# Causal attention on VectorE, TensorE and GpSimd: the sine product taken from PSUM, the products of the key chunks set apart, the last three for both heads at once

## The chip, the cores and the metric

The kernel runs on one core of one Trainium2 chip. The metric is the device time of one execution in microseconds (us). The engines carry the profile's names: PE is TensorE (PEld its weight loads), DVE is VectorE, ACT is ScalarE, POOL is GpSimd, and SP is the queue that issues most DMAs.

## The reference, cut to what matters

Everything is fp32. The input x is 4 batches of 1024 rows of 256. An attention with 16 heads of 64, rotary positions and a causal mask comes first, then a residual and a layer norm, then a mixture of 16 experts (3 for each row) with another residual and norm. The change touches the attention alone:

```python
q = _rope(q, sin, cos)
k = _rope(k, sin, cos)
att = jnp.einsum('bhqd,bhkd->bhqk', q, k) * scale      # scale = 1/8
att = jnp.where(mask, att, -inf)
att = softmax(att)
y = jnp.einsum('bhqk,bhkd->bhqd', att, v)
return y @ W_out.T + b_out
...
y_lo = x_lo * cos + x_hi * sin                          # in _rope
y_hi = x_hi * cos - x_lo * sin
```

So a rotated q or k is the projection times a sine table plus the projection with its halves swapped times a cosine table.

## The kernel before, in words

**Tiling.** The attention runs over 32 pairs n: 4 batches times 8 pairs of heads. The two heads of a pair lie in partitions 0 to 63 and 64 to 127. Queries and keys of a batch are 8 chunks of 128 each. A pair has six slots k, and its query chunks come from the longest row to the shortest, `chunks = [(7,), (6,), (5,), (4,), (3, 2), (1, 0)]` (L410): query chunk 7 sees 8 key chunks, query chunk 0 sees one.

**The steps of a pair.** In the slots of the pair before it, `project` (L200) makes q and k, transposed: two matmuls of 512 columns for each half of the positions (L214), then an activation of ScalarE from PSUM to SBUF that adds the bias and, for q, multiplies by SCALE (L218). SP then copies the tile with its 32-row halves swapped (four DMAs, L230). `rotate` (L232) multiplies the projection by the sine table where it stands (L236: on DVE for q, on POOL for k), the swapped copy by the cosine table (L242, POOL), and adds (L245, POOL). `values` (L247) makes v for two pairs at once (L254), copies it out of PSUM (L259, ScalarE) and stores it to a DRAM scratch (L264, SP); `spread` (L271) loads it back as vr with 32 keys of each of four groups on the partitions.

`scores` (L279) multiplies one or two query chunks with all keys that they see (L300, tiles of 64 rows and 128 columns, one for each head), DVE adds the mask and takes the row's extreme from PSUM into SBUF (L308), and ScalarE takes exp with the row's sum (L320). `divide` (L331) takes the reciprocal of the sum on DVE (L334) and multiplies on POOL (L337). Two slots later `turn` (L346) transposes the probabilities in 32x32 blocks on DVE (L357) into two tiles: t_first for key chunks 0 to 3 and t_last for 4 to 7. Each has one buffer.

`product` (L364) does one key chunk j of probabilities times values for all query chunks from j on: 4 blocks u of 32 queries, 2 heads, 4 blocks a of 32 keys, each a matmul with a 32x64 tile of vr as weights and 32 (8 - j) columns (L378); chunk 7 leaves 12 of the 32 out. The trace records each fp32 matmul as two MATMUL and two LDWEIGHTS. The results stay in four PSUM tiles y_ps, one for each a, until all chunks are added. `close` (L386) adds the bias of v and joins the four tiles into yT with four activations of ScalarE (L391), and `out` (L397) multiplies yT with the output weights (L400), a quarter of the rows a call; DVE adds that to the residual (`sum`, L455).

**What sets the order.** PE's instructions stand in the order of the program (`manual_schedule`, L427). Within slot k of pair n they are: for k = 2 the product of chunks 1 and 0 of the pair before and its close; the scores; for k = 0 and 1 the products of chunk 4 and of chunks 3 and 2 of the pair before, for k = 3, 4, 5 those of chunk 7, 6, 5 of this pair; an `out` in slots 0, 3, 4, 5; the projections of the next pair, K0, K1, Q1, Q0 in slots 0 to 3 (0 and 1 are halves of the positions); values in slots 4 and 5. The other engines take what is ready by the order of the program, which `after` (L327) ties with dependencies that mean order alone: the sum behind the first head's transposes, the reciprocals behind the second's, the sine multiplication of q behind the transposes, POOL's rotations behind the divides. The rotation of k is written in slot 2, that of Q1 in slot 3, of Q0 in slot 5.

**PSUM.** [...]four (ps_s) go round among scores, projections, values, out and the router, four (ps_y) hold y_ps. A PE tile in ps_s waits until its buffer's reader is done.

**The MoE part.** The router of a batch (layer norm, routing, table scatters) is spread over slots of later pairs by `plan`; the experts run behind the attention.

## Time and profile before

| what | us |
|---|---|
| median of 3 runs | 1808.53 (1807.02 to 1809.19) |
| the profiled execution | 1897.37 |
| its span | 1895.6 |
| PE busy with matmuls | 1671.1 |
| POOL, DVE, ACT busy | 1191.2, 1169.3, 713.4 |
| mean of a scores reduction L308 over 512 columns without a row so far | 0.685 |
| mean of a transpose L357 | 0.588 |
| mean of an exp L320 | 0.766 |
| mean of a divide L337 | 0.769 |
| mean of a projection matmul L214 | 0.622 |

The span is what the profile covers, 1.8 us less than its execution. Durations of PE rows overlap[...]: how long a step takes is read from the start of one step to the start of the next. A wait in brackets behind a row of a timeline is the idle time before it with the instruction that ended it.

### The profile page before, as it was taken

Reading aid. Unit: us, or ns where it says so; the run is one execution under the profiler, and the core shown is the slowest. Engines: PE = TensorE matmul, PEld = TensorE weight load, DVE = VectorE, ACT = ScalarE, POOL = GpSimd, SP = SyncE. Lnnn points to the kernel's source line nnn. Section 1 sums busy time; section 2 is a strip of 40 time slices with the busy share of each in tenths; the row PEclk is TensorE's granted clock in tenths of the full one; section 3 lists DMA queues with packets and bytes.
Section 4 is the critical chain, followed back from the end, with each engine's and each line's share of the span. In section 5 each row is a group of like instructions: output and inputs, shape, how many; then the busy total and the mean of one; then the engine's idle time right before and its main releaser. Section 6 shows DMA issues by size and latency. Waiting matters only on the chain.

```text
span 1895.6 us, 51958 instructions
## 1 busy us (share of the span) xinstructions
PE 1671.1 (88%) x20920; PEld 1141.3 (60%) x20920; DVE 1169.3 (62%) x3458; ACT 713.4 (38%) x1634; POOL 1191.2 (63%) x1077
## 2 busy tenths in 40 slices
PE   7899999988989898899999798898779799999980
PEld 3466556555555565555555465554458588888870
DVE  4687788868766787886668778766625122223224
ACT  3445454544344444444345443343312122222223
POOL 3776577655667775556776655577536778777542
PEclk9899999999999998999999998999879899999995
DMA  6365445463444556345444643343367689888856
GB/s 178 92 162 141 115 117 128 117 187 94 116 99 98 109 124 184 91 122 115 99 107 99 193 100 92 84 95 90 93 219 192 143 239 249 234 237 228 219 94 266
DMA packets 118168, 272.97 MB, mean 144 GB/s; under 512 B 21874, under 2 KB 72434, under 8 KB 102563
## 3 DMA queue, kind: packets, MB, share of 16 engines
q1 hardware_dynamic: 93122, 239.91, 46.2%
q0 software_dynamic: 24656, 29.68, 8.9%
q8 instruction: 167, 2.74, 0.7%
q14 instruction: 79, 0.64, 0.1%
q10 hardware_dynamic: 144, 0.01, 0.0%
HBM read 183.17 MB, written 52.79 MB: 124 GB/s over the span
## 4 chain that ended last, share of the span: by engine, by line
PE 59%; DVE 17%; issue 10%; DMA 7%; SPq 3%; ACT 2%; POOL 1%; ACTq 0%; DVEq 0%; POOLq 0%
PE y_ps L378 16%; PE ps L874 10%; PE ps L890 10%; PE s L300 8%; PE pp L214 6%; PE oo L400 4%; DVE p L308 4%; DVE t_first L357 4%; PE vv L254 3%; SPq L230 3%; DMA swq<-rotq 3%; DVE t_last L357 3%; ACT p L320 1%; PE ps L862 1%; DVE acc L455 1%
## 5 line engine op out<-in xcount | busy, mean ns | idle before, releaser
L337 POOL TENSOR_SCALAR p<-p,rinv 128x512 f32<-128x512 f32 (+7 forms) x512 | 385.8, 769 | 450.6 <-DVE rinv L334 446.4
L320 ACT ACTIVATE p<-p,nmax 128x512 f32<-128x512 f32 (+7 forms) x512 | 392.0, 766 | 474.2 <-DVE nmax L308 415.8
L300 PE MATMUL s<-rotk,rotq 64*128 64x512 f32 (+3 forms) x1536 | 343.0, 533 | 44.5 <-DVE x2T L578 17.1
L308 DVE CUSTOM_DVE_ANT_0 p<-s,zero 128x512 f32<-128x512 f32 x256 | 165.8, 685 | 246.7 <-PE s L300 242.0
L300 PEld LDWEIGHTS s<-rotk,rotq 64*128 64x128 f32 x1536 | 160.8, 193 | 232.0 <-issue 102.6
L357 DVE STREAM_TRANSPOSE t_first<-p 128x512 f32<-128x512 f32 (+3 forms) x512 | 288.9, 588 | 0.9 <-POOL p L337 0.9
L378 PE MATMUL y_ps<-t_first,vr 32*64 32x160 f32 (+2 forms) x8192 | 250.9, 348 | 28.4 <-issue 25.2
L214 PE MATMUL pp<-xT,wqk 128*128 128x512 f32 x512 | 254.6, 622 | 16.4 <-DVE nmax L308 8.8
L378 PEld LDWEIGHTS y_ps<-t_first,vr 32*64 32x64 f32 x8192 | 181.0, 134 | 110.1 <-issue 79.6
L904 POOL DMA_INDIRECT sums<-y,ids x112 | 178.5, 1594 | 72.2 <-DVE y L900 37.8
L879 ACT ACTIVATE hid<-ps,w 128x256 f32<-128x256 f32 x224 | 93.7, 471 | 333.7 <-issue 264.4
L874 PE MATMUL ps<-xg,w 128*128 128x256 f32 x896 | 210.8, 387 | 8.6 <-issue 5.7
L895 DVE TENSOR_TENSOR y<-ps,w 128x512 f32<-128x512 f32 x56 | 38.7, 691 | 286.5 <-PE ps L890 215.6
L890 PE MATMUL ps<-w,hid 128*128 128x256 f32 x896 | 203.9, 380 | 1.9 <-issue 1.8
L874 PEld LDWEIGHTS ps<-xg,w 128*128 128x128 f32 x896 | 169.6, 195 | 33.3 <-issue 9.1
L890 PEld LDWEIGHTS ps<-w,hid 128*128 128x128 f32 x896 | 169.6, 190 | 25.6 <-issue 2.8
L400 PE MATMUL oo<-wo,yT 128*128 128x256 f32 x512 | 153.4, 425 | 32.9 <-DVE nmax L308 31.3
L378 PE MATMUL y_ps<-t_last,vr 32*64 32x96 f32 (+3 forms) x7424 | 148.4, 257 | 32.9 <-DVE t_last L357 16.3
L378 PEld LDWEIGHTS y_ps<-t_last,vr 32*64 32x64 f32 x7424 | 116.5, 137 | 95.7 <-issue 54.0
L214 PEld LDWEIGHTS pp<-xT,wqk 128*128 128x128 f32 x512 | 94.6, 195 | 109.7 <-issue 67.6
L308 DVE CUSTOM_DVE_ANT_0 p<-s,mask,nmax 128x512 f32<-128x512 f32 (+3 forms) x256 | 130.3, 545 | 0.9 <-issue 0.5
L254 PE MATMUL vv<-wv,xT 128*128 128x256 f32 x512 | 130.1, 401 | 0.0
(150 smaller groups left out, 1985.4 us busy)
## 6 DMA issues: line engine op xcount, KB each, us to landing
vr<-v_d SPq DMA_DIRECT2D x256, 256.0 KB
w<-in_wall_dram SPq DMA_DIRECT2D x56, 1154.0 KB
swq<-rotq SPq DMA_DIRECT2D x256, 64.0 KB
swk<-rotk SPq DMA_DIRECT2D x128, 128.0 KB
v_d<-v SPq DMA_DIRECT2D x128, 128.0 KB
wqk<-in_w_qk_dram SPq DMA_DIRECT2D x32, 256.0 KB
xT<-in_xT_dram SPq DMA_DIRECT2D x8, 512.0 KB
wv<-in_w_v_dram SPq DMA_DIRECT2D x16, 256.0 KB
```

The costliest lines, as they stand in the source:

```text
L214: nc.tensor.matmul(ps, lhsT=wqk[n][:, c, i, :], rhs=xts[b, g][:, c, :], start=(c == 0), stop=(c == DC - 1),)
L254: nc.tensor.matmul(ps[:, u, :], lhsT=xts[b, cc // 2][:, c, ts(cc % 2 * 2 + u, P)], rhs=wv[n][:, c, :], start=(c == 0), stop=(c == DC - 1),)
L300: nc.tensor.matmul(s[:, :n_k], lhsT=rot[n, 0, qc // 4][ts(hh, KD), ts(qc % 4, P)], rhs=k[ts(hh, KD), ds(k0, n_k)], start=True, stop=True,)
L308: order["scores"] = nc.vector.tensor_tensor_reduce(out=probs[n, qc, hh][:, ds(k0, n_k)], in0=s[:, :n_k], in1=mask[:, 512 - n_k :] if last ...
L320: nc.scalar.activation(pr, pr, AF.Exp, bias=m, scale=-1.0, accum_out=rsum[:, hh : hh + 1])
L337: order["divide"] = router.behind = nc.gpsimd.tensor_scalar(pr, pr, rinv[:, hh : hh + 1], 1.0, ALU.mult, ALU.mult)
L357: order["turn"] = router.on_dve = after(nc.vector.transpose(t[:, hh, :, ds(i - 4 * h, n_j, step=step), :], pr[:, ds(512 * h, n_j * P)].rea ...
L378: nc.tensor.matmul(st[n][a][ts(hh, KD), ds(32 * j, 32 * (TC - j))], lhsT=vrs[n, h][ts(a, 32), jh // 2 * 8 + 2 * u + jh % 2, ts(hh, KD)], r ...
L400: nc.tensor.matmul(ps[:, v, :], lhsT=st[n][:, ts(2 * h + v, P)], rhs=wo[n], start=True, stop=True,)
L874: nc.tensor.matmul(ps[:, f - f0, :], lhsT=w[:, ds(c * FF + f * P, P)], rhs=xg[:, c, :], start=(c == 0), stop=(c == DC - 1),)
L890: nc.tensor.matmul(ps[:, h, :], lhsT=hid[:, f, ts(h, P)], rhs=w[:, ds(W2_AT + f * D, D)], start=(f == 0), stop=(f == FC - 1),)
L904: s = behind(nc.gpsimd.indirect_dma_start(out=sums[t % 2], out_offset=bass.IndirectOffsetOnAxis(ap=ids[:, h, i : i + 1], axis=0), in_=y[:, ...
```

## The change

The change has four parts.

1. The sine product is made by DVE straight from the projection's PSUM tile: (projection + bias) x sine in one operation, into the tile of the rotated q or k, ordered behind the reciprocal of the slot. ScalarE's activation still copies projection plus bias to SBUF, now into a tile of its own (`raw`), and only the swap DMAs read that. `rotate` keeps the cosine product and the sum. The scale of the scores moves from q into the reduction on DVE, and the mask is divided by it.
2. The projections are K0, K1, Q1 in slots 0 to 2 and Q0 in slot 5. Q1 is rotated in slot 4, Q0 in slot 0 of its own pair. Values go from slots 4 and 5 to 3 and 4. For pair 0, values of two tiles go from ahead of the loop to its slots 1 and 2, and the first projections are in another order.
3. No two key chunks follow each other on PE: slot 0 has the scores, chunk 4, out, a projection, chunk 3; slot 1 the scores, chunk 2, a projection; slot 2 chunk 1, the scores, chunk 0, the close, a projection. The transposes are ordered by halves of the keys: both heads' t_last, the sum, both heads' t_first.
4. Chunks 7, 6 and 5 (WIDE = 3) use 32x128 tiles of vr with both heads as weights and both heads' probabilities as columns: half as many matmuls with twice the columns. In the result, the quarter that pairs a head's values with its own probabilities is kept for each head; the cross terms land in the other quarters of y_ps, which now uses 512 columns, and are not read. The close has eight activations of 64 partitions.

```diff
...
         rot = {}
-        swps = {}
+        raws, swps = {}, {}
         def project(n, i, g):
             b, p = divmod(n, NP)
             if i == 0:
-                res = rot[n, 0, g] = qkp.tile([P, 512], FP, tag=f"rotq{g}", name="rotq")
-                half, whole = res, True
+                half = rot[n, 0, g] = qkp.tile([P, 512], FP, tag=f"rotq{g}", name="rotq")
+                part = raw = qkp.tile([P, 512], FP, tag="rawq", name="rawq")
+                whole = True
             else:
                 whole = (n, 1) in rot
                 if not whole:
                     rot[n, 1] = qkp.tile([P, T], FP, tag="rotk", name="rotk")
-                res = rot[n, 1]
-                half = res[:, ts(g, 512)]
+                    raws[n] = qkp.tile([P, T], FP, tag="rawk", name="rawk", bufs=1)
+                half, raw = rot[n, 1][:, ts(g, 512)], raws[n]
+                part = raw[:, ts(g, 512)]
             ps = ps_s.tile([P, 512], FP, tag="s", name="pp")
             for c in range(DC):
                 nc.tensor.matmul(
                     ps, lhsT=wqk[n][:, c, i, :], rhs=xts[b, g][:, c, :],
                     start=(c == 0), stop=(c == DC - 1),
                 )
-            nc.scalar.activation(
-                half, ps, AF.Identity,
-                bias=(bq_s if i == 0 else bqk[:, 1, :])[:, p : p + 1],
-                scale=SCALE if i == 0 else 1.0,
+            bias = bqk[:, i, p : p + 1]
+            nc.scalar.activation(part, ps, AF.Identity, bias=bias)
+            m = nc.vector.scalar_tensor_tensor(
+                half, ps, bias, sin[:, ts(g, 512)], ALU.add, ALU.mult
             )
+            if n:
+                after(m, "inverse")
             if whole:
                 if i == 0:
...
                 else:
                     swp = swps[n, 1] = qkp.tile([P, T], FP, tag="swk", name="swk", bufs=1)
                 for r in range(4):
-                    nc.sync.dma_start(out=swp[ts(r, 32), :], in_=res[ts(r ^ 1, 32), :])
+                    nc.sync.dma_start(out=swp[ts(r, 32), :], in_=raw[ts(r ^ 1, 32), :])
         def rotate(n, i, g=None):
             key = (n, i) if i else (n, i, g)
             swp, res = swps.pop(key), rot[key]
-            at = slice(None) if i else ts(g, 512)
-            first = (nc.gpsimd if i and n else nc.vector).tensor_tensor(
-                res, res, sin[:, at], ALU.mult
+            eng = nc.vector if n == 0 and i else nc.gpsimd
+            first = eng.tensor_tensor(
+                swp, swp, cos if i else cos[:, ts(g, 512)], ALU.mult
             )
-            if n:
-                after(first, "divide" if i else "turn" if "turn" in order else "scores")
-            eng = nc.vector if n == 0 and i else nc.gpsimd
-            second = eng.tensor_tensor(swp, swp, cos[:, at], ALU.mult)
-            if n:
-                after(second, "divide")
+            if "divide" in order:
+                after(first, "divide")
             eng.tensor_tensor(res, res, swp, ALU.add)
         def values(n, cc):
...
                         start=(c == 0), stop=(c == DC - 1),
                     )
             nc.scalar.copy(v.rearrange("p i u d -> p u i d"), ps.rearrange("p u (i d) -> p u i d", i=2))
-            if cc == 0:
+            if n // 2 not in vds:
                 vds[n // 2] = v_d.tile([NG, 2, 32, 2, 4, 2 * P], FP, tag="v_d", name="v_d")
             for i in range(2):
...
         probs = {}
-        def scores(n, qcs):
+        def scores(n, qcs, kind=None):
             k = rot[n, 1]
             parts = []
...
             for qc, hh, k0, n_k, s in parts:
                 last = k0 + n_k == (qc + 1) * P
                 m = sp.tile([P, 1], FP, tag=f"nmax{hh}", name="nmax")
-                order["scores"] = nc.vector.tensor_tensor_reduce(
+                i = nc.vector.tensor_tensor_reduce(
                     out=probs[n, qc, hh][:, ds(k0, n_k)], in0=s[:, :n_k],
-                    in1=mask[:, 512 - n_k :] if last else zero[:, :n_k], scale=1.0,
+                    in1=mask[:, 512 - n_k :] if last else zero[:, :n_k], scale=SCALE,
                     scalar=3e38 if k0 == 0 else nmax[qc, hh],
                     op0=ALU.add, op1=ALU.min, accum_out=m,
                 )
                 nmax[qc, hh] = m
+                if kind:
+                    after(i, kind)
+                order["scores"] = i
                 if last:
                     pr = probs[n, qc, hh]
                     if hh == 0:
...
         def divide(n, ends, kind):
             for qc, rsum in ends:
                 rinv = sp.tile([P, 2], FP, tag="rinv", name="rinv")
-                after(nc.vector.reciprocal(rinv, rsum), kind)
+                order["inverse"] = after(nc.vector.reciprocal(rinv, rsum), kind)
                 for hh in range(2):
                     pr = probs[n, qc, hh]
                     order["divide"] = router.behind = nc.gpsimd.tensor_scalar(
...
         turned = {}
-        def turn(n, i, hh, kind):
+        def turn(n, i, hh, h, kind):
             if n not in turned:
                 turned[n] = (
                     tp.tile([P, 2, 4, 29, 32], FP, tag="first", name="t_first"),
                     tp.tile([P, 2, 4, 13, 32], FP, tag="last", name="t_last"),
                 )
-            pr = probs.pop((n, i, hh))
-            for h, (t, step) in enumerate(zip(turned[n], (7, 3))):
-                n_j = min(4, i + 1 - 4 * h)
-                if n_j <= 0:
-                    continue
-                order["turn"] = router.on_dve = after(nc.vector.transpose(
-                    t[:, hh, :, ds(i - 4 * h, n_j, step=step), :],
-                    pr[:, ds(512 * h, n_j * P)].rearrange("p (j u q) -> p u j q", u=4, q=32),
-                ), kind)
+            n_j = min(4, i + 1 - 4 * h)
+            order["turn"] = router.on_dve = after(nc.vector.transpose(
+                turned[n][h][:, hh, :, ds(i - 4 * h, n_j, step=7 - 4 * h), :],
+                probs[n, i, hh][:, ds(512 * h, n_j * P)].rearrange("p (j u q) -> p u j q", u=4, q=32),
+            ), kind)
         st = {}
         def product(n, j):
             if j == TC - 1:
...
             t = turned[n][h]
             at = jh * (8 - 4 * h)
             for u in range(4):
-                for hh in range(2):
+                for hh in ([0, 1] if j < TC - WIDE else [None]):
                     for a in range(4):
                         if j == TC - 1 and a < u:
                             continue
+                        y = st[n][a].rearrange("p (h q) -> p h q", h=2)[:, :, 32 * j : 32 * TC]
+                        v = vrs[n, h][ts(a, 32), jh // 2 * 8 + 2 * u + jh % 2, :]
+                        pt = t[ts(a, 32), :, u, ds(at, TC - j), :]
+                        if hh is not None:
+                            y, v, pt = y[ts(hh, KD), hh, :], v[:, ts(hh, KD)], pt[:, hh]
                         nc.tensor.matmul(
-                            st[n][a][ts(hh, KD), ds(32 * j, 32 * (TC - j))],
-                            lhsT=vrs[n, h][ts(a, 32), jh // 2 * 8 + 2 * u + jh % 2, ts(hh, KD)],
-                            rhs=t[ts(a, 32), hh, u, ds(at, TC - j), :],
+                            y, lhsT=v, rhs=pt,
                             start=(j == TC - 1 and u == 0), stop=(j == 0 and u == 3),
                             skip_group_check=True,
                         )
...
             yT = yp.tile([P, TC, 4, 32], FP, tag="yT")
             for a, y in enumerate(st.pop(n)):
-                nc.scalar.activation(
-                    yT[:, :, a, :], y[:, : 2 * P].rearrange("p (i q) -> p i q", q=32),
-                    AF.Identity, bias=bv[:, p : p + 1],
-                )
+                for hh in range(2):
+                    at = ts(hh, KD)
+                    nc.scalar.activation(
+                        yT[at, :, a, :], y[at, ts(hh, 2 * P)].rearrange("p (i q) -> p i q", q=32),
+                        AF.Identity, bias=bv[at, p : p + 1],
+                    )
             st[n] = yT.rearrange("p i a q -> p (i a q)")
         def out(n, h):
...
         chunks = [(7,), (6,), (5,), (4,), (3, 2), (1, 0)]
         n_slots = len(chunks)
         n_pairs = B * NP
-        for i, g in ((1, 0), (0, 0), (1, 1), (0, 1)):
+        for i, g in ((1, 0), (1, 1), (0, 1), (0, 0)):
             project(0, i, g)
-        for cc in range(4):
+        rotate(0, 1)
+        rotate(0, 0, 1)
+        for cc in (2, 3):
             values(0, cc)
-        rotate(0, 1)
-        for g in (1, 0):
-            rotate(0, 0, g)
         load_rest()
         plan = {}
         first = []
...
                 if n == 2:
                     load_router()
                 for k in range(n_slots):
-                    m, js = (n - 1, ((4,), (3, 2), (1, 0))[k]) if k < 3 else (n, (10 - k,))
-                    if k == 2 and one_of(m):
-                        for j in js:
-                            product(m, j)
-                        close(m)
-                    ends = scores(n, chunks[k]) if one_of(n) else []
-                    if k != 2 and one_of(m):
-                        for j in js:
-                            product(m, j)
-                    part = None
+                    here, before = one_of(n), one_of(n - 1)
+                    part, ends = None, []
+                    if k == 2 and before:
+                        product(n - 1, 1)
+                    if here:
+                        ends = scores(n, chunks[k])
+                    if k < 3 and before:
+                        product(n - 1, (4, 2, 0)[k])
+                        if k == 2:
+                            close(n - 1)
+                    if k >= 3 and here:
+                        product(n, 10 - k)
                     if k in (0, 3, 4, 5) and one_of(n - 1 - (k == 0)):
                         part = out(n - 1 - (k == 0), (k - 3) % 4 if k else 3)
                     m, kk = divmod(n * n_slots + k - 2, n_slots)
+                    rows = [(qc, h) for h in (1, 0) for qc in chunks[kk] if qc >= 4 * h]
                     last = "scores"
-                    for hh in range(2):
+                    for i, (qc, h) in enumerate(rows):
                         if one_of(m):
-                            for qc in chunks[kk]:
-                                turn(m, qc, hh, last)
-                            last = "turn"
-                        if hh == 0 and part:
+                            for hh in range(2):
+                                turn(m, qc, hh, h, last)
+                                last = "turn"
+                        if i == 0 and part:
                             a, ps = part
                             order["sum"] = after(nc.vector.tensor_tensor(a, ps, a, ALU.add), last)
                             last = "sum"
...
                         late(load_qk(n + 2))
                     if one_of(n + 1):
-                        if k < 4:
-                            project(n + 1, *((1, 0), (1, 1), (0, 1), (0, 0))[k])
+                        if k in (0, 1, 2, 5):
+                            project(n + 1, int(k < 2), int(k in (1, 2)))
                         if k == 2:
                             rotate(n + 1, 1)
-                        elif k in (3, 5):
-                            rotate(n + 1, 0, int(k == 3))
+                        elif k == 4:
+                            rotate(n + 1, 0, 1)
+                    if k == 0 and one_of(n):
+                        rotate(n, 0, 0)
+                    if k == 0 and before:
+                        product(n - 1, 3)
                     m = n + 2 - n % 2
-                    if k in (4, 5) and one_of(m):
-                        values(m, 2 * (n % 2) + k - 4)
+                    if k in (3, 4) and one_of(m):
+                        values(m, 2 * (n % 2) + k - 3)
+                    if k in (1, 2) and n == 0:
+                        values(0, k - 1)
                     if k in (0, 4):
                         if n < 2 and k == 4 * (1 - n):
                             residual(0, n)
```

## The prediction

> **What bounds the kernel now.** I read the page first: engine shares and the costliest groups. Then what PE waits for, then the timelines of the four engines over one undisturbed head pair (115.26 to 151.93 us, 36.67 us), then the same views where PE stands still longest.
>
> ```profile
> PE 1671.1 (88%) x20920; PEld 1141.3 (60%) x20920; DVE 1169.3 (62%) x3458; ACT 713.4 (38%) x1634; POOL 1191.2 (63%) x1077
> q8 instruction: 167, 2.74, 0.7%
> ```
> PE is the bound: 88% busy, the others about 60%. Attention ends near 1396 us; the MoE behind it is untouched. So the change is worth what PE's own work in a pair, and PE's waits, become. The waits:
>
> ```profile
> PE y_ps L378 <- issue: 32.4, 67, 2.6
> PE oo L400 <- DVE nmax L308: 31.3, 23, 1.5
> PE s L300 <- DVE x2T L578: 17.1, 3, 6.6
> PE s L300 <- ACT rotq L218: 10.4, 28, 0.4
> ```
> The second and third lines have one cause, the sine multiplication L236 on DVE. In the undisturbed pair (DVE, then PE):
>
> ```profile
> 129.26 2.23 DVE L236 TENSOR_TENSOR rotq<-rotq,sin 128x512 f32<-128x512 f32 x1 [0.31 <-DMA swq<-rotq]
> 131.42 0.68 DVE L308 CUSTOM_DVE_ANT_0 p<-s,mask 128x512 f32<-128x512 f32 x1
> ```
> ```profile
> 128.09 1.77 PE L300 MATMUL s<-rotk,rotq 64*128 64x512 f32 x8
> 129.80 0.91 PE L378 MATMUL y_ps<-t_last,vr 32*64 32x64 f32 x64
> 132.15 1.13 PE L400 MATMUL oo<-wo,yT 128*128 128x256 f32 x4 [1.44 <-DVE nmax L308]
> ```
> The sine multiplication overwrites the tile that the swap DMAs read, so it waits for them, and the slot's reductions (L308) queue behind it; PE's next tile then has no free PSUM buffer: 1.44 us. In a pair that also normalises it is worse:
>
> ```profile
> 739.58 0.96 DVE L236 TENSOR_TENSOR rotq<-rotq,sin 128x512 f32<-128x512 f32 x1 [5.27 <-DMA swq<-rotq]
> ```
> The swap came 5.27 us late there; the x2T copy stood behind it, and PE idled 5.10 us. The three normalise pairs have 5.39 + 5.10 + 6.57 = 17.1 us of that.
>
> The first line of the waits ("issue") lies inside long product bursts. The burst of chunks 1 and 0 takes 3.43 to 3.50 us in undisturbed pairs, but up to 9.3 in nine pairs with table scatters:
>
> ```profile
> 553.47 0.97 PE L378 MATMUL y_ps<-t_first,vr 32*64 32x224 f32 x21
> 557.09 3.38 PE L378 MATMUL y_ps<-t_first,vr 32*64 32x224 f32 x48 [2.65 <-issue]
> ```
> Over all pairs the excess of these bursts is 58.3 us, that of chunk 5's bursts 13.4, that of the last pair's tail 23: 94.7. The profiled execution took 1897.37 us, 88.8 more than the median of 1808.53. Without the 94.7 it would be 1802.7, so most of these stalls look like something of the profiled execution, and at most 1808.53 - 1802.7 = 5.8 us of them is left over by this reckoning. My sum is therefore a difference, built from rows free of them, and added to the median.
>
> [...] L236 takes 0.66 us at best, but 2.23 here, under a POOL operation that runs 128.59 to 130.95. The sum L455, one input from PSUM, stays at a mean of 0.66. [...] the trace of before has no 32x128 operation. [...] The q8 line agrees on the size (2.74 MB / 167 = 16 KB). Two such packets fall into the window of the slow burst above[...]: the stalls may be late fetches.
>
> **The change part by part.** Start-to-start steps are from the pair's PE timeline.
>
> Sine from PSUM: L236 goes. DVE gets four PSUM-source operations of about 0.66 us a pair (from L455), 2.6 us, instead of two of 0.66 to 2.6; POOL loses a 128x1024 operation, 2.37 us. The new ones stand behind the slot's reciprocal, wait for PE only, and never for the swap. Behind them on DVE queue the next slot's reductions; 0.66 us fits in DVE's idle time (4.56 us before slot 2's reductions, 0.4 to 0.7 elsewhere), so I price it at nothing; uncovered it would be 0.66 a slot. Gains: the 1.44 us in slot 4, and the 17.1 us. The late swap now holds POOL's cosine multiplication instead, but that stands a slot (about 7 us) later for q1 and about a slot and a half for q0, more than the 5 to 7 us of lateness.
>
> Products apart. A burst obeys 0.31 us + 0.1015 ns per column (8192 columns 1.14, 22528 2.60, 30720 3.43 us; two chunks in one burst pay the 0.31 once). Splitting by columns alone: chunk 3 1.18, 2 1.42, 1 1.60, 0 1.83. The change adds two bursts a pair. Chunk 0's lies beside slot 3's wait, below. Chunk 3's, between a projection and scores[...]: between nothing and 0.31, I take half, 0.15.
>
> Slots: slot 0 was 5.84, + 1.18 + 0.15 = 7.17. Slot 1 was 6.21, - 2.60 + 1.42 = 5.03. Slot 2: 1.60 + 1.56 scores + 1.83 + 1.91 projection = 6.90.
>
> Slot 3's new wait. Let s be the start of slot 2's scores. ScalarE's two exps start at s + 2.97 (118.69 to 121.66) and end at s + 4.82; then close, now eight 64x256 activations at the measured step of 0.39 = 3.12, and the raw copy 0.67: the projection's PSUM buffer is free at s + 8.6. PE asks for it with the last scores tile at s + 1.56 + 1.83 + 1.91 + 1.34 = s + 6.64. So PE waits about 2.0 us, where before it waited 0.37, because close came ahead of the exps. Were close half that (four operations' worth), the wait would be 0.4; were the 64-partition ones dearer than 0.39, longer. Slot 3 is then (8.6 - 5.3) + 0.41 + chunk 7 + out 0.97 + values 1.82. Wide chunk 7: 0.45 (half the instructions, the columns doubled) to the 0.67 of before; I take 0.45, so 6.95.
>
> Slots 4 and 5 (u the start of slot 4's scores): without L236 ahead, DVE reduces to u + 3.1, transposes and sums to u + 5.6, and the reciprocals end at u + 5.9; POOL divides 2.48 and rotates q1 2.6 (1.27 + 1.28): the next pair's first scores at about u + 11.05. PE's own work: scores 1.71, out 0.97, values 1.82, scores 0.85, out 0.97, projection 1.81, and wide chunks 6 (0.85 to 1.14) and 5 (1.28 to 1.56): 10.3 to 10.8, hidden under POOL with 0.25 to 0.75 to spare. Before: 6.85 + 4.94 = 11.79.
>
> Sum: 7.17 + 5.03 + 6.90 + 6.95 + 11.05 = 37.10, against 36.67: **+0.43 a pair**, x 32 = +13.8. So the 1.44 and the small waits are spent again in slot 3 and on the split.
>
> Moved: values go a slot earlier with their copy and two v_d stores each; Q0's projection with its four swap DMAs goes to slot 5, on SP's queue behind the vr loads of slot 4 and the next weights; needed in slot 4 of the next pair, some 20 us later: nothing. Pair 0: two values tiles leave the start; its first scores come about 4.1 us earlier, the tiles cost 3.6 in slots 1 and 2, and PE's 2.2 us wait for vr goes: -2.7.
>
> Total: +13.8 - 17.1 - 2.7, and of the burst stalls, of which up to 5.8 us seem to be there and whose bursts get smaller (168 of some 1170 recorded PE instructions a pair less, and none of the longest left), -4: **-10.0**. 1808.5 - 10 = **1798.5**. The profiled execution's own time, 1897.4, should fall by more, as its stalls lie in these bursts.
>
> **Rivals.** *Slower.* PE pays in full for its added work: chunk 3's entry 0.31 (+0.16), wide chunk 7 at 0.67 (+0.22), and wide chunks 5 and 6 at 1.56 + 1.14, 0.85 over before, 0.6 of it covered (+0.25). That is +1.06 a pair, +34 in all, - 17.1 - 2.7: 1822.7. It decides from (17.1 + 2.7) / 32 = 0.62 a pair. For it: PE is 88% busy, and products are paced by columns. Against: POOL covers most of slots 4 and 5. *Much faster.* The stalls are late instruction fetches and exist without the profiler: then half of the 94.7 goes with the long bursts, -40 or so on my sum without the -4, less some of it in other places: 1768. For it: the fetches in the slow burst's window. Against: the arithmetic of 88.8. *No change.* The normalise pairs' 17 us come back as waits for a late swap on POOL, whose divides queue behind it; the pair's +0.43 shrinks to +0.1 (no entry, close partly hidden): 1808.5 + 3 - 2.7 = 1809.
>
> **How the numbers follow.** Forecast 1798.5, itself between 1787 and 1806 (pair +0.28 to +0.55, stalls 0 to -10): chance 0.43. Much faster 0.18, no change 0.13, slower 0.26. About 0.2% (3.6 us) is what a measurement of this kernel can tell from no change. Faster by more than that: 0.40 of the forecast + 0.18 = 0.58; within: 0.03 of the forecast + 0.11 of no change = 0.14; slower: the other 0.02 + 0.26 = 0.28. Range from 1766, leaving out half of "much faster", to 1824, leaving out the tail of "slower".
>
> **What would show it.** L236 gone from DVE, 128 PSUM-source operations of 0.66 us in its place; the 31.3 us of out waiting for nmax and the 17.1 for x2T gone. New: some 2 us of scores waiting on ScalarE in slot 3 of each pair, scores of slot 0 waiting on POOL's rotq by 0.2 to 0.7, 256 close operations of 0.39 step. Wrong if wide chunk 5 takes over 1.6 us, if the waits for x2T return as waits on POOL, or if the median falls by more than 25: then the burst stalls were real.

## The result, and the profile after

The changed kernel takes **1874.12 us** (median of 4, 1870.15 to 1880.05), the kernel before 1808.86 (1807.02 to 1812.67): a ratio of 1.036, with a 95% interval of 1.034 to 1.038. It is slower by 65 us where 10 us less were forecast, and far above the range's upper end of 1824. The profiled execution took 1874.21 us (span 1872.4).

That the profiled execution and the median agree here, but lay 88.8 us apart before, needs one remark. Chips differ: the kernel before took 1804 to 1809 us in three groups of runs and 1882 to 1893 in four others, and the two chips that were used twice gave the same sort both times. The chip of its first profile is not on record, but with 1897 us and 32.4 us of "issue" in PE's long bursts that profile looks like the second sort, while its times are of the first. On the second sort these bursts stall (31.6 us in before_again, 14 in after_again); on the first hardly (none listed in the profile after, 2.9 us in split_again). The profile after is of the first sort. All ratios below are to the kernel before on the same chip, and each is marked with the sort.

What PE waits for, after (engine, tile and line, releaser: us in total, times, longest):

```profile
PE s L300 <- POOL rotq L245: 56.1, 29, 5.5
PE y_ps L386 <- ACT yT L399: 18.0, 33, 1.1
PE s L300 <- DVE nmax L308: 17.1, 30, 0.6
PE pp L216 <- DVE nmax L308: 11.0, 4, 3.6
```

The four waits shown of before (issue, out on nmax, scores on x2T, scores on ScalarE's copy) are gone from this list. Four others stand in their place, 102 us against 91. The first lies at slot 0, the next two in slot 3, the fourth in slot 1 of the normalise pairs. PE's timeline in slot 3 of an undisturbed pair, and the start of its slot 4:

```profile
124.35 1.34 PE L300 MATMUL s<-rotk,rotq 64*128 64x512 f32 x6
126.27 0.48 PE L300 MATMUL s<-rotk,rotq 64*128 64x128 f32 x2 [0.57 <-DVE nmax L308]
126.68 0.55 PE L386 MATMUL y_ps<-t_last,vr 32*128 32x64 f32 x6
127.78 1.10 PE L386 MATMUL y_ps<-t_last,vr 32*128 32x64 f32 x14 [0.55 <-ACT yT L399]
128.81 1.18 PE L408 MATMUL oo<-wo,yT 128*128 128x256 f32 x4
129.78 3.57 PE L254 MATMUL vv<-wv,xT 128*128 128x256 f32 x8
133.28 1.77 PE L300 MATMUL s<-rotk,rotq 64*128 64x512 f32 x8
...
137.06 1.89 PE L254 MATMUL vv<-wv,xT 128*128 128x256 f32 x8
```

There are two short waits, 1.12 us together. The row at 129.78 is the surprise: the same eight matmuls of values take 3.57 us there and 1.89 at 137.06, with no wait in either. The view by stretches (length, then busy time of PE, its weight loads, DVE, ScalarE and POOL, then the granted clock) says why:

```profile
126.20:129.80 3.60, 2.99 (x27) 2.55 (x28) 1.96 (x10) 2.38 (x6) 3.52 (x3) 0.99 0.03 8
129.80:133.30 3.50, 3.50 (x11) 2.33 (x9) 2.73 (x6) 1.51 (x4) 2.27 (x2) 0.52 0.30 71
133.30:139.00 5.70, 5.70 (x55) 4.16 (x56) 4.56 (x13) 3.32 (x10) 0.90 (x2) 1.00 0.40 109
```

For one stretch of 3.41 us after the waits, from 129.75 to 133.16, the granted clock is 0.50 (1.00 ahead of it and behind it), and the eight matmuls take 1.68 us more. It follows two waits of 0.57 and 0.55 us inside busy work; why the clock falls, the trace does not say.

It does show in which pairs it falls. The 77 changes of the granted clock in this trace lie whole multiples of 3.413 us apart, to 0.002 us, as if on marks at that distance; the slots do not: the first mark behind the first scores of slot 3 comes 0.02 to 3.06 us after them. Where no mark lay between the start of the first wait and the end of the second, the stretch from the next mark on was at half clock, in all of 15 pairs. Where a mark lay between the waits or early in the second, 2.3 to 3.1 us after the slot's first scores, none of 9 pairs had it. With the mark inside the first wait or just behind it (1.7 to 2.0 us) five of six had it; the sixth has no second wait. So whether a pair of this run pays goes with where its slot 3 lies between the marks.

Length of slots in us, from one slot's first scores to the next, read from PE's timeline. The undisturbed pair at full clock (for after, slot by slot, since hardly a pair has all of them undisturbed):

| kernel | slot 0 | 1 | 2 | 3 | 4 | 5 | pair |
|---|---|---|---|---|---|---|---|
| before | 5.83 | 9.64 | 3.83 | 5.58 | 6.85 | 4.94 | 36.67 |
| after | 7.13 | 6.80 | 5.32 | 7.24 | 5.59 | 5.55 | 37.63 |
| split alone | 7.13 | 6.80 | 5.32 | 5.54 | 5.39 | 4.62 | 34.80 |

and the sums over pairs 1 to 30, all on chips of the first sort:

| kernel | slot 0 | 1 | 2 | 3 | 4 | 5 | all |
|---|---|---|---|---|---|---|---|
| after | 240 | 227 | 161 | 267 | 167 | 215 | 1276 |
| after, waits filled | 236 | 226 | 162 | 231 | 167 | 219 | 1241 |
| split alone | 252 | 220 | 162 | 174 | 190 | 163 | 1162 |
| split and sine | 241 | 220 | 165 | 214 | 178 | 153 | 1171 |

In 21 of the 30 pairs, slot 3 of the changed kernel is over 8.5 us; undisturbed, it is about 7.2 or about 8.9, and nothing between. A half-clock stretch starts in slot 3 in 20 of them.

### The profile page after: what moved, and what is told of

It reads as the page before. It is cut to its first block, busy times and chain, and to the rows that moved or that the text cites. A ratio compares the mean times of both kernels' runs of the same rounds, so it can differ in the third digit from the quotient of the medians.

```text
span 1872.4 us, 46638 instructions
## 1 busy us (share of the span) xinstructions
PE 1687.6 (90%) x18232; PEld 1170.7 (63%) x18232; DVE 1171.9 (63%) x3520; ACT 781.1 (42%) x1762; POOL 1096.0 (59%) x1046
## 4 chain that ended last, share of the span: by engine, by line
PE 69%; DVE 10%; POOL 8%; DMA 5%; issue 4%; ACT 3%; SPq 1%; POOLq 0%; ACTq 0%; DVEq 0%
PE y_ps L386 14%; PE s L300 13%; PE ps L891 10%; PE ps L907 10%; PE pp L216 10%; PE oo L408 4%; PE vv L254 4%; POOL p L340 3%; ACT yT L399 2%; DVE p L308 2%; DVE t_first L357 2%; POOL rotq L245 2%; POOL swq L240 2%; DMA wqk<-in_w_qk_dram 2%; PE ps L879 1%
## 5 line engine op out<-in xcount | busy, mean ns | idle before, releaser
L340 POOL TENSOR_SCALAR p<-p,rinv 128x512 f32<-128x512 f32 (+7 forms) x512 | 374.0, 745 | 563.4 <-DVE rinv L337 553.0
L300 PE MATMUL s<-rotk,rotq 64*128 64x512 f32 (+3 forms) x1536 | 341.3, 540 | 74.9 <-POOL rotq L245 56.1
L357 DVE STREAM_TRANSPOSE t_first<-p 128x512 f32<-128x512 f32 (+3 forms) x512 | 275.6, 580 | 0.6 <-POOL p L340 0.5
L386 PE MATMUL y_ps<-t_first,vr 32*64 32x160 f32 (+1 forms) x8192 | 218.8, 345 | 3.0 <-DVE t_first L357 2.7
L386 PEld LDWEIGHTS y_ps<-t_first,vr 32*64 32x64 f32 x8192 | 161.7, 133 | 86.7 <-DVE t_first L357 34.5
L891 PE MATMUL ps<-xg,w 128*128 128x256 f32 x896 | 204.5, 382 | 3.7 <-DVE xg L881 3.7
L386 PE MATMUL y_ps<-t_last,vr 32*64 32x128 f32 (+3 forms) x4736 | 189.4, 305 | 19.7 <-ACT yT L399 18.0
L386 PEld LDWEIGHTS y_ps<-t_last,vr 32*128 32x128 f32 (+1 forms) x4736 | 155.9, 170 | 81.1 <-issue 48.3
L408 PE MATMUL oo<-wo,yT 128*128 128x256 f32 x512 | 161.5, 444 | 7.8 <-ACT yT L399 3.9
L254 PE MATMUL vv<-wv,xT 128*128 128x256 f32 x512 | 145.7, 437 | 0.0
L308 DVE CUSTOM_DVE_ANT_0 p<-s,mask 128x512 f32<-128x512 f32 (+3 forms) x256 | 112.2, 486 | 37.6 <-PE s L300 37.4
```

The costliest lines, as they stand in the source:

```text
L254: nc.tensor.matmul(ps[:, u, :], lhsT=xts[b, cc // 2][:, c, ts(cc % 2 * 2 + u, P)], rhs=wv[n][:, c, :], start=(c == 0), stop=(c == DC - 1),)
L300: nc.tensor.matmul(s[:, :n_k], lhsT=rot[n, 0, qc // 4][ts(hh, KD), ts(qc % 4, P)], rhs=k[ts(hh, KD), ds(k0, n_k)], start=True, stop=True,)
L308: i = nc.vector.tensor_tensor_reduce(out=probs[n, qc, hh][:, ds(k0, n_k)], in0=s[:, :n_k], in1=mask[:, 512 - n_k :] if last else zero[:, : ...
L340: order["divide"] = router.behind = nc.gpsimd.tensor_scalar(pr, pr, rinv[:, hh : hh + 1], 1.0, ALU.mult, ALU.mult)
L357: order["turn"] = router.on_dve = after(nc.vector.transpose(turned[n][h][:, hh, :, ds(i - 4 * h, n_j, step=7 - 4 * h), :], probs[n, i, hh] ...
L386: nc.tensor.matmul(y, lhsT=v, rhs=pt, start=(j == TC - 1 and u == 0), stop=(j == 0 and u == 3), skip_group_check=True,)
```

## The experiments

The theories: **G**, the half-clock stretches behind short waits of PE; **S**, the sine operation, which waits for ScalarE's copy; **W**, the wide products, with their close of eight operations; **M**, the moved slots. In tables and ratios, (1) is a chip without stalls in long bursts, (2) one with them.

| run | ratio to before | 95% interval | chip |
|---|---|---|---|
| after | 1.036 | 1.034 to 1.038 | (1) |
| after_again | 1.032 | 1.027 to 1.037 | (2) |
| close_first | 1.053 | 1.043 to 1.063 | (2) |
| narrow8 | 1.022 | 1.011 to 1.032 | (2) |
| fill | 1.073 | 1.063 to 1.084 | (2) |
| sin_only | 1.011 | 1.007 to 1.015 | (2) |
| wide_only | 1.020 | 1.013 to 1.026 | (2) |
| split_only | 0.962 | 0.958 to 0.967 | (2) |
| narrow4 | 1.010 | 1.004 to 1.017 | (2) |
| sine_first | 1.058 | 1.050 to 1.066 | (2) |
| narrow4_sine_first | 1.021 | 1.015 to 1.027 | (2) |
| wide_shared | 1.021 | 1.016 to 1.026 | (2) |
| fill_gap | 1.021 | 1.018 to 1.024 | (1) |
| split_sine | 0.974 | 0.972 to 0.975 | (1) |
| split_sine_first | 0.972 | 0.970 to 0.974 | (1) |
| split_again | 0.970 | 0.967 to 0.972 | (1) |
| split_sine_first_again | 0.972 | 0.969 to 0.975 | (1) |
| q1_slot3 | 1.010 | 1.000 to 1.021 | (2) |

**The kernel before again**, no edit.

> The kernel of before, unchanged, under the profiler once more. In its first profile the long product bursts lost 94.7 us, and its execution took 1897 us where the median is 1808. If those stalls belonged to that one execution, this one takes about 1808, and the burst of chunks 1 and 0 takes 3.4 us in all pairs. If the profiler makes them each time, it takes about 1897 again.

It took 1897.76 us, with 31.6 us of "issue" in PE's bursts, beside runs of the kernel before with a median of 1882 on that chip. So the stalls belong neither to one execution nor to the profiler: the two groups of experiments on a chip of sort (1) ran at 1809 and 1804.

**close_first**, two places:

```diff
+                        product(n - 1, 0)
+                        close(n - 1)
...
-                        product(n - 1, (4, 2, 0)[k])
-                        if k == 2:
-                            close(n - 1)
+                        product(n - 1, (4, 2)[k])
```

> The changed kernel, with the products of chunks 1 and 0 and the close together ahead of slot 2's scores, as before; all else is kept. Theory G (the close now stands behind slot 2's two exps on ScalarE; PE stands still about 1.1 us in slot 3 and then runs one stretch of 3.4 us at half clock in about 20 of 32 pairs, 1.7 us each): the waits (35 us in all) and the slow stretches (34) go: 1874 - 60 to 70, about 1810. Rival W (the wide products themselves, with their doubled columns, cost it): within 10 us of 1874. Rival S (the sine operation, which holds PSUM buffers until ScalarE's raw copy is done): a small gain, 1860 to 1870.

It took 1979 us, about 2% more than the changed kernel. The theory as written fell: an earlier place of the close does not help. PE's last scores of slot 3, then ScalarE's and DVE's rows ahead of it:

```profile
171.75 0.48 PE L300 MATMUL s<-rotk,rotq 64*128 64x128 f32 x2 [2.35 <-DVE rotq L222]
```
```profile
164.35 3.87 ACT L399 ACTIVATE yT<-y_ps,bv 64x256 f32<-64x256 f32 x8 [2.76 <-PE y_ps L386]
...
170.22 0.69 ACT L221 ACTIVATE rawq<-pp,bqk 128x512 f32<-128x512 f32 x1
```
```profile
170.94 0.75 DVE L222 SCALAR_TENSOR_TENSOR rotq<-pp,bqk,sin 128x512 f32<-128x512 f32 x1 [0.55 <-ACT rawq L221]
171.61 0.68 DVE L308 CUSTOM_DVE_ANT_0 p<-s,zero 128x512 f32<-128x512 f32 x1
```

The eight operations now delay the exps as well, then the copy, then the sine; and slot 3's reductions stand behind the sine.

**narrow8**: `WIDE = 0`.

> The changed kernel with all products narrow (WIDE = 0); y_ps keeps its layout by head halves, so the close still has eight operations. Theory G: within 10 us of 1874, for the close stays where it is, and the wide products of chunks 5 and 6 lie beside POOL's chain. Rival W: the products take 0.26 + 0.53 + 0.3 us less a pair, 30 us or more off: about 1840. Rival S: 1874.

1.022 against 1.032 (after_again, below, on another chip of the same sort), with intervals that overlap. Narrow products with the same close give back about 1%, at the edge of the noise: W's products are at most a part.

**fill**: the matmuls of Q1's projection in slot 2 twice.

```diff
-            for c in range(DC):
+            for c in list(range(DC)) * (2 if n and (i, g) == (0, 1) else 1):
```

> The changed kernel with the matmuls of the Q1 projection in slot 2 made twice, into the same tile with the same values: 1.9 us of PE work more in each pair, in the place just ahead of PE's wait in slot 3. Theory G, its part on the clock: the added work fills the idle time, the half-clock stretch of slot 3 goes, and the time falls by up to 34 us in spite of the added work: 1840 to 1860. If the clock is not the cause and only the waits count: 1874 plus 0 to 30 (1.9 us of work, about 1.1 of it in place of the wait).

It missed both: 1.073. DVE's row shows what it did instead of a test of the clock:

```profile
216.39 0.75 DVE L222 SCALAR_TENSOR_TENSOR rotq<-pp,bqk,sin 128x512 f32<-128x512 f32 x1 [3.71 <-ACT rawq L221]
```

The longer projection put the sine ahead of slot 3's reductions in DVE's order, where it waited 3.71 us for the copy. It says nothing on G, and much on S. Why the sine waits for ScalarE at all, when both only read the PSUM tile, no trace shows; that it does, the profile of the changed kernel shows in both lines, 98.5 us in all.

```profile
DVE rotq L222 <- ACT rawq L221: 58.7, 50, 1.6
DVE rotk L222 <- ACT rawk L221: 39.8, 55, 8.5
```

**The parts alone**, each put into the kernel before, with the changed kernel on the same chip.

> The changed kernel itself, on the same chip as the three parts below, for in the first experiments the kernel of before took 1882 us on its chip instead of 1808. Its ratio to before should again be about 1.036, if the long bursts' stalls do not differ; if they are there on this chip and the smaller bursts relieve them, it falls to about 1.00.

> The kernel before, with part 1 alone: the sine product on DVE straight from PSUM, the copy for the swap by ScalarE, the scale in the reduction; slots, products and close as before. Theory S (the sine operation waits for ScalarE's copy of the same PSUM bank, and DVE's queue waits with it; this hurts where the copy is late, which it is here only a little, since the close has four operations and comes first): faster, -1.4 us in slot 4 of each pair and -17 at the normalisations, +0.4 in slot 3: about -45 us, ratio 0.975. If the sine operation is harmful by itself: ratio 1.00 to 1.02.

> The kernel before, with the wide products of chunks 7, 6 and 5 alone and so with eight close operations. The close takes 3.9 us instead of 1.6, and everything on ScalarE behind it (the exps of slot 2, the copy of Q1) comes about 2 us later; products cost 0.3 to 0.9 us more a pair. Theory S and W both: slower by 1.5 to 2.5 us a pair, ratio 1.025 to 1.045; if the wide products are harmless: 1.00.

> The kernel before, with the products set apart alone (and the transposes ordered by halves), close of four operations behind chunk 0. The close stands behind slot 2's exps, so ScalarE's copy of Q1 is 1.6 us later than the exps: slot 3 waits 0.7 us instead of 0.4[...]: +0.5 us a pair, ratio 1.01, or, where long bursts stall on this chip, a gain of up to half of those stalls: 0.98.

The changed kernel kept its ratio, 1.032. The sine alone was forecast as a gain of 2.5% by theory S and costs 1.1%. Its forecast gains came: out's wait for nmax fell from 30.7 us (before_again) to 0.7, the three waits for x2T went, and slot 4 is 59 us shorter in sum. But slot 3 is 55 us longer, slot 1 24 and slot 5 15. PE waits 34.4 us in slot 3 for the sine operation, and in slots 1 and 4 the scores themselves are longer (sin_only, then the split alone as split_again; PE, the last scores of slot 3 and the scores of slot 4):

```profile
126.14 0.48 PE L299 MATMUL s<-rotk,rotq 64*128 64x128 f32 x2 [1.26 <-DVE rotq L221]
131.70 2.54 PE L299 MATMUL s<-rotk,rotq 64*128 64x512 f32 x8
```
```profile
160.12 1.77 PE L300 MATMUL s<-rotk,rotq 64*128 64x512 f32 x8
```

The 0.77 us more appear in no list of PE's waits; in split_sine, where the same scores also take 2.54 us (158.99 to 161.53), the granted clock is 1.00 from 158 to 162. The two heads' tiles run side by side in the split, with starts within 0.01 us of each other. In sin_only the second head's last tile starts 0.67 us behind the first head's, and its weight load shows what it waited for: it takes the PSUM buffer of the projection, which the sine operation reads until 133.28:

```profile
133.34 0.29 PEld L299 LDWEIGHTS s<-rotk,rotq 64*128 64x128 f32 x2 [0.48 <-DVE rotq L221]
```

The wide products cost 2.0%, short of the expected 2.5 to 4.5. The split, forecast at 0.98 to 1.01, gains 3.8%; it includes the new order of the transposes, which was not tried apart. Its slots 4 and 5 show that the wait of out for nmax, 1.44 us in every undisturbed pair, goes with the split alone too, though L236 is still there (DVE, POOL, PE):

```profile
162.12 0.75 DVE L236 TENSOR_TENSOR rotq<-rotq,sin 128x512 f32<-128x512 f32 x1 [0.84 <-DMA swq<-rotq]
```
```profile
159.97 2.36 POOL L242 TENSOR_TENSOR swk<-swk,cos 128x1024 f32<-128x1024 f32 x1
162.40 2.70 POOL L245 TENSOR_TENSOR rotk<-rotk,swk 128x1024 f32<-128x1024 f32 x1
```
```profile
160.93 1.77 PE L300 MATMUL s<-rotk,rotq 64*128 64x512 f32 x8
162.64 0.94 PE L375 MATMUL y_ps<-t_last,vr 32*64 32x64 f32 x64
163.53 1.13 PE L397 MATMUL oo<-wo,yT 128*128 128x256 f32 x4
```

Chunk 0's burst now stands between slot 2's scores and slot 4, so PE reaches slot 4 some 1.5 us later against POOL's chain. POOL's cosine product starts 0.96 us before slot 4's scores, where it started 0.50 after (128.59 against 128.09), so L236, which meets only the last 0.21 us of that operation, takes 0.75 us instead of 2.23. (In the profile before, L236 took 2.61 to 2.63 us in the 17 of its 64 instances that had L242 beside their first 2.06 to 2.08 us, and 0.68 at 23.99 with POOL idle.) One and the same wait can thus be removed by the sine or by the split, and counts once.

**Close, sine order, and both**. narrow4 takes `product` and `close` as before. sine_first exchanges two statements:

```diff
-            nc.scalar.activation(part, ps, AF.Identity, bias=bias)
             m = nc.vector.scalar_tensor_tensor(
                 half, ps, bias, sin[:, ts(g, 512)], ALU.add, ALU.mult
             )
+            nc.scalar.activation(part, ps, AF.Identity, bias=bias)
```

wide_shared is wide_only with head 1's close as `nc.vector.tensor_scalar_add(yT[at, :, a, :], src, bv[at, p : p + 1])`.

> The changed kernel with part 4 undone: all products narrow, y_ps and the close of four operations as before. Split, sine from PSUM and the moved slots stay. Theory S (what costs is ScalarE's longer close ahead of the copy of Q1, and the sine operation and PSUM bank behind that copy): the close ends 2.3 us earlier, slot 3 waits about 1.2 us instead of 2: about 36 us a pair, ratio to before 0.98. If part 4 is harmless and the sine alone is guilty: ratio 1.02 to 1.03 as in the changed kernel.

> The changed kernel with one swap: DVE's sine operation is written ahead of ScalarE's copy, so that ScalarE waits for DVE and not DVE for ScalarE. Nothing else differs. Theory S: DVE's 98 us of waiting for the copies go, its queue moves on, and the bank is free 0.7 us earlier after the copy: 0.6 to 1.2 us a pair less, ratio to before about 1.01 instead of 1.032. If the order of the two does not matter: 1.03.

> Both of the last two together: narrow products, close of four operations, sine ahead of the copy. Theory S: what is left of the change is the split, which alone gave 0.962, and a sine operation that costs no wait: 0.95 to 0.97. If the sine from PSUM or the moved slots cost by themselves: above 0.975.

> The kernel before with the wide products alone, and the eight close operations shared: head 0's four on ScalarE, head 1's four on DVE, which stands idle at that time. If the length of the close on ScalarE is what made wide products cost 1.020: slot 3 falls back to about 5.8 us from 7.1 to 8.8, ratio about 1.00. If the wide products themselves cost it: 1.02 again.

narrow4 gave 1.010: wide products and close together are worth about 2.2%, and slot 3 falls to 6.34 us, 8.0 where the clock falls. But it did not reach the 0.98 that S expected, for slots 4 and 5 still take 11.16. sine_first is a plain miss, 1.058. DVE no longer waits for ScalarE, but ScalarE waits 207 us for DVE, slot 3 keeps its two waits, and slot 0 takes 8.18 us in 15 of 30 pairs. There the clock is full (1.00), but the scores take 3.04 us instead of 1.99, because the second head's last tile again starts late (its weight load waits 0.76 us). With a close of four operations, the same exchange brings slot 3 to 5.71, yet the ratio is 1.021: slot 0 again. wide_shared has slot 3 at 6.1 us, as expected, but the ratio stays at 1.021, which by its own terms speaks for the wide products. The slots say otherwise: against wide_only, slot 3 falls by 63 us in sum while slots 2 and 4 grow by 31 and 30, where a projection and out now wait for DVE's reductions (32.1 and 16.2 us), which stand behind its four operations of the close. So a long close costs on either engine here; how much of the 2% is the products' own columns stays open.

**fill_gap**, the clock by itself; **split_sine**, **split_sine_first**, for the moved slots.

```diff
-                        nc.tensor.matmul(
+                        for _ in range(4 if qcs == (4,) and k0 else 1): nc.tensor.matmul(
```

> The changed kernel, with the two 128-column score matmuls of slot 3 made four times each instead of once, with the same values into the same tiles: about 1.2 us of work on PE in the two places where it waits, 0.57 and 0.55 us. If the half-clock stretches come from these waits: slot 3 takes 7.2 to 7.6 us in nearly all pairs, instead of 8.9 in most, and the ratio to before falls from 1.032 to about 1.018. If the waits have nothing to do with the clock: slot 3 keeps its 8.9 in most pairs, ratio 1.03 to 1.05.

> The kernel before with the split and the sine from PSUM, old slots, narrow products, close of four operations. If the moved slots are what costs 1.15 us in slots 4 and 5 (POOL's chain): those two slots together take about 10.0 us, slot 3 about 6.4 as in narrow4 (with 8.0 where the clock falls), ratio about 0.98, against 1.010 of narrow4. If the sine alone is guilty: 1.01.

> The same with the sine operation written ahead of ScalarE's copy. Slot 3 about 5.7 us as in narrow4_sine_first, slots 4 and 5 about 10.0, no x2T wait at the normalisations: ratio 0.955 to 0.965, as good as the split alone (0.962) or better. If the sine costs in other slots: 0.97 or more.

fill_gap does more work and takes 1843 us, 31 less than the changed kernel on a chip of the same sort (before: 1809 on both). Slot 3 of an undisturbed pair:

```profile
156.65 3.07 PE L300 MATMUL s<-rotk,rotq 64*128 64x512 f32 x20
159.65 1.52 PE L386 MATMUL y_ps<-t_last,vr 32*128 32x64 f32 x20
161.10 1.13 PE L408 MATMUL oo<-wo,yT 128*128 128x256 f32 x4
162.07 1.89 PE L254 MATMUL vv<-wv,xT 128*128 128x256 f32 x8
```

Values follow in 1.89 us (the granted clock is 1.00 from 155 to 165). Slot 3 takes 7.24 us in most pairs and over 8.5 in 8 instead of 21; its sum falls by 35 us, and half-clock stretches start in it in 5 pairs instead of 20. **Theory G holds for slot 3**: the waits' own 1.12 us stay (as work), what goes is most of the half clock behind them. The five that stay have no wait of PE in front of them, so idle time is not all that counts; what else does was not tried. split_sine missed its 0.98 by a little to the better side (0.974), split_sine_first was expected better than that and is not. Both have slots 4 and 5 at 10.7 to 11.0, not at 10.0: slot 4's scores take 2.54 and 2.82 us instead of 1.77, at a granted clock of 1.00 (split_sine 158 to 162, split_sine_first 160 to 166), as long as in sin_only or longer, where the second head's last tile starts 0.67 us late.

**The split again, beside the split with the sine.**

> The split alone, once more. If this chip shows no stalls in the long bursts (the kernel of before about 1809 us): the clean pair is 1.85 us shorter than before (34.8 against 36.7), 30 us in most pairs, some more from the waits at the normalisations: ratio 0.965 to 0.975. If it shows them (about 1885): 0.96 again.

> The split with the sine ahead of the copy, on the same chip as split_again. Its clean pair is 36.0 us against 34.8 of the split alone, and only the three normalisations speak for it: slower than the split alone by 10 to 25 us.

0.970 and 0.972: the split alone is worth 52 us without any stalls to relieve, and the sine from PSUM, even in its better order, adds nothing measurable to it. The expected 10 to 25 us between the two were not there (3.5). Either beats both kernels, 1751 and 1755 us against 1804.

**q1_slot3**, the changed kernel with one number back:

```diff
-                        elif k == 4:
+                        elif k == 3:
                             rotate(n + 1, 0, 1)
```

> The changed kernel with the rotation of Q1 written in slot 3 again instead of slot 4; nothing else differs. If the late rotation costs the time in slots 4 and 5: PE's 56 us of waiting for rotq at slot 0 go, slot 5 takes 5.2 to 5.6 us in most pairs, and the ratio to before falls from about 1.034 to about 1.005 to 1.015. If not (the wait only moves to slot 4's divides, or to the swap): 1.03.

1.010 (1.000 to 1.021) against 1.032 (1.027 to 1.037; after_again, another chip of the same sort). PE's wait for rotq falls from 69.8 to 5.4 us (after_again, then q1_slot3), the sum of slot 5 from 238 to 171, while slot 0's grows from 236 to 261.

```profile
PE s L300 <- POOL rotq L245: 69.8, 29, 5.1
```
```profile
PE s L300 <- POOL rotq L245: 5.4, 2, 3.2
```

**Theory M holds** for the rotation of Q1: this one step costs about 2%, 40 us. The other moved slots were not put back one by one.

## Why the prediction was wrong, point by point

- *The sine waits for PE only and is priced at nothing.* Wrong. It waits for ScalarE's copy from the same PSUM tile, 98.5 us in all, and DVE's queue with it. Its duration was right within 0.1 us (0.75 against 0.66). In split_sine, slot 3 is 0.8 us longer for it (6.33 against 5.54) and slot 4 0.7 (6.10 against 5.39).
- *The 1.44 us in slot 4 is the sine's gain.* Right as to the wait: sin_only removes it (30.7 us to 0.7). But the split removes it alone too, and the sine pays for it in slots 1, 3 and 4. The split alone takes 10.0 us in slots 4 and 5, so beside it the forecast 11.05 is a loss of 1 us, while against before it is a gain of 0.74.
- *Slots 4 and 5 take 11.05, PE's work hidden under POOL.* Right for an undisturbed pair (11.14), and POOL's chain is the bound there, as forecast. What was missed is that the chain does not start on time elsewhere: scores of slot 0 wait up to 5.5 us for rotq where 0.2 to 0.7 was forecast, 56.1 us in all. In pairs with router work on DVE the reciprocals come late, and Q1's rotation, a slot later than before, comes late with them (POOL, then PE, at the end of pair 10):

```profile
468.03 2.62 POOL L340 TENSOR_SCALAR p<-p,rinv 128x512 f32<-128x512 f32 x4 [10.46 <-DVE rinv L337]
470.62 1.26 POOL L240 TENSOR_TENSOR swq<-swq,cos 128x512 f32<-128x512 f32 x1
471.96 1.26 POOL L245 TENSOR_TENSOR rotq<-rotq,swq 128x512 f32<-128x512 f32 x1
```
```profile
473.28 2.93 PE L300 MATMUL s<-rotk,rotq 64*128 64x512 f32 x6 [4.30 <-POOL rotq L245]
```

- *The 17.1 us of the normalise pairs.* The x2T wait is gone, as forecast, and nothing is gained by it. The first normalise pair and the two behind it took 46.43 + 44.80 + 42.86 = 134.1 us before and 46.85 + 45.87 + 46.52 = 139.2 after. Slot 4 gives 8.5 us in the first, 0.7 in the second and 5.5 in the third. Slot 3 takes back 3.3, 1.6 and 5.0, slots 0 to 2 together 5.1, nothing and 1.9, and slot 5 0.5, 0.2 and 2.3. In the first, slot 1 has a wait of 3.56 for nmax (the fourth line of the waits). POOL waited only once for a swap of q; what took the gain back were the new waits. (The profile before is of the second sort, so these differences are rough.)
- *Slots 0 to 2.* Nearly right: 19.10 forecast, 19.25 measured at best, 19.30 before. The 19.30 hold a wait of 0.35 us of slot 2's projection for nmax, which goes with the split; without it PE's steps were 18.95, so the two added bursts cost 0.30 together, where 0.15 was forecast. In the first pairs slot 0 takes 7.5 to 8.0 us, not 7.13: its scores wait for rotq (0.34 us at 100.21), and the second head's last tile starts 0.26 us behind the first's (101.43 against 101.17).
- *Slot 3 waits about 2 us, 6.95 in all.* Half right: ScalarE's close of eight, 3.86 us instead of 3.12, does hold back PE, but not through the projection's buffer as forecast. The last scores wait 0.57 us for a reduction on DVE, and chunk 7 waits 0.55 for y_ps, which the close reads. That is 1.12 us instead of 2, but wide chunk 7 takes 1.07 us (in close_first, without a wait), not 0.45: 7.24. **Missing altogether was what follows a wait**: the half-clock stretch, 1.69 us in two of three pairs, 31 us by fill_gap, nearly as much as the two waits themselves (35 us).
- *Wide chunks 5 and 6.* 1.51 and 1.11, inside the bounds.
- *The start, -2.7.* Right in sign: the first scores come 4.5 us earlier, pair 1's 5.0.
- *The burst stalls.* That they belong to the profiled execution was wrong, they belong to the chip. On sort (1) there was nothing to relieve (none listed in the profile after), so the rival of 1768 was out; on sort (2) the changed kernel still has 14 us of them, against 31.6. Smaller bursts relieve little: from sort (1) to sort (2) the kernel before loses 73 to 89 us, the changed kernel 76 and the split alone 68, about 40 of them in slot 2 for the last two (161 to 201 and 162 to 199 in sum), where the burst of chunk 0 lies. What makes these chips slower stays open.

The failing step is the pair's +0.43, and in it three terms that were put at nothing. The sine operation was priced at nothing because it was to "wait for PE only"; it waits for ScalarE's copy, and alone costs 1.1%. The new wait in slot 3 was priced at its length alone; half a clock follows it in 20 of 30 pairs, 31 us. And POOL's chain was given its undisturbed length in every pair; with Q1's rotation a slot later it costs about 2% (q1_slot3). At full clock the pair is +0.96 (37.63 - 36.67), 17 us more than forecast over 32 pairs; the rest is the half clock and the longer waits ahead of slot 0. The 17.1 us of the normalise pairs, counted in full, were spent again. Seen from the best version, on chips of sort (1), the account by slots is clearer: the changed kernel's pairs take 114 us more than the split's (1276 - 1162), of which +93 in slot 3 and +52 in slot 5, -23 in slot 4 and -12 in slot 0. The slower rival had the sign and, at +1.06, nearly the undisturbed pair (+0.96), with added bursts and chunk 7 among its reasons; but at 1822.7 it too had no term for the half clock and the late chain, which carried most of the rest. How the 114 us divide exactly is open: the parts are not additive (sine_first), and narrow4 and q1_slot3 ran on chips of sort (2) alone. Not tried was a sine operation that reads another PSUM tile than the copy.

## What to carry to other kernels

A change made of several parts is priced against the kernel with each part alone: here one part carried the whole gain (0.970), and a wait that two parts each remove (out's for nmax) counts once. Before a second engine is given the same PSUM tile, count it as a place in the first engine's queue, with everything queued behind it (here 98.5 us of DVE waiting for the copy, 207 us of ScalarE waiting with the order exchanged), and count the PSUM buffer as taken until both have read it (in sin_only the next weight load waited 0.48 us for the sine). A delay can also hide in the scores, where no idle time of PE is listed (2.54 us instead of 1.77), so compare an operation's own length before and after. And price a new wait of the bounding PE not at its length alone, but allow for a stretch at half clock behind it (here 1.69 us behind 1.12 us of waits); whether that stretch comes can be tried by filling the wait with repeated matmuls (20 pairs with it became 5 in fill_gap).

## What the runs showed of the hardware that was not expected

- Two waits of 0.57 and 0.55 us within 2 us were followed by a stretch at half clock (0.50) in 20 of the 29 pairs of the changed kernel that have both, of 3.41 us in 14 of them and 6.83 in six. It came in every one of the 15 where both lay between two neighbouring marks, 3.413 us apart, of the clock's changes in that trace, so an undisturbed slot 3 takes 7.24 or 8.93 us. Length of idle time alone does not decide: the 21 waits of out in the profile before, 1.36 to 1.46 us each, drew none, 12 of them wholly between two neighbouring marks of that trace.
- The two heads' score tiles of slot 4 start within 0.01 us of each other in the split. Where the second head's last tile had to wait for its PSUM buffer, it started 0.67 us behind, and the scores took 2.54 us instead of 1.77, with no idle time of PE listed (sin_only, slot 4); in split_sine they take the same 2.54 us at a granted clock of 1.00.
- The same kernel differs by 4 to 5% between chips (1804 to 1809 against 1882 to 1893), in part by stalls in PE's long bursts that no wait explains (31.6 us in before_again). A profile and a median taken on different chips can't be set against each other.
- More work can be faster: fill_gap's 1.2 us of repeated matmuls a pair took 31 us off.
